# A quantized, low-rank-adapted double matrix product: another order for one strip's side work on TensorE, ScalarE and GpSimd

## The chip, the cores and the metric

The kernel runs on one core of one Trainium2 chip. The metric is device time in microseconds (us) of one execution. Before the change the median of 3 runs is 2667.78 us (2667.24 to 2671.78).

## What is computed

The reference, cut to what matters (x is 4096 tokens by 2048 in float32; `weight`, `W_base` are 2048 by 2048; the codebook has 32 values; lora rank 64; router of 8 experts with rank 16):

```python
lora_delta = lora_B @ lora_A * (32.0 / 64.0)
cb = codebook / max(abs(codebook))
wg = (weight + lora_delta).reshape(O, I // 128, 128)
normalized = wg / exp(scale_log)
quantized = cb[searchsorted((cb[:-1] + cb[1:]) * 0.5, normalized)]
w_q = ((quantized - normalized) + normalized) * exp(scale_log)
h = x @ (w_q + lora_delta).T                 # the conditioning layer
out = x + h @ W_base.T + b_base + 2.0 * routed_lora(h, A_w, cores, B_w, router_w)
```

`routed_lora` mixes 16 by 16 cores with a softmax over 8 experts. Nothing lies between the two large products but linear algebra, so the kernel first multiplies the two weight matrices (and adds the identity for the residual), and then multiplies x by the result.

## The kernel before, in words

**Two stages.** Stage A makes the combined weights, 16 *strips* of 128 input columns one after the other (`for i in range(NS)`, L755). Stage B (L873 on) multiplies x by them in 4 groups of 1024 tokens, each as 7 by 7 smaller products (two levels of a Strassen-like scheme) whose operands lie in `s_dram`. Stage A writes the combined strip blocks to `wc_dram`, and forms and writes the sums of blocks that stage B needs to `s_dram`.

**One strip of stage A** is a tile `w` of 128 by 2048 floats, normalized, and a tile `a` of the same size that becomes the quantized strip. The codebook has 31 thresholds. For a threshold r from 4 on, `raise_to` (L544) does two full-width instructions: ScalarE writes a *mask* of one byte per element (L549), VectorE then copies the next codebook value into `a` where the mask is set (L550). That is 27 mask steps; in what follows Mk is the step with r = 4 + k, so M0 to M26. There are 4 mask buffers (`mpool`, L431), so ScalarE can be at most four masks ahead of VectorE. From strip 6 on half of threshold 3 is one more, half-wide step in front of M0 (L556-557). The first codebook values and thresholds of a strip are made beforehand, during the strip before it, by other passes: ScalarE's three passes L516, L519 and L521 or L524 on a half strip (`scalar_level`), and GpSimd's pairs L534, L535 (`pool_levels`) and L539 (`last_level`).

**Side work during strip i.** The list `at` holds calls; `behind(k, f, ...)` has f's instructions recorded after the two instructions of Mk. Every engine runs its own instructions strictly in that recorded order (`tc.manual_schedule()`, L367); only semaphores hold engines against each other. The side work of strip i is:

- for strip i + 1: `load_w` (L391, two loads on SyncE's queue; there are two `w` tiles, so the tile is free only when strip i - 1 has read its `w` for the last time), `delta` (L404, the low-rank product of one half, 16 matmuls into the one PSUM tile `d`), `scaled` (L498, ScalarE takes `d` out into `a`, L502), `normalize` (L504, GpSimd adds it to `w`, L506, and divides, L429), then the first levels as above;
- for strip i - 1: `straight_through` (L564) has just been recorded behind M26 of strip i - 1: GpSimd does L572, L573, L574 on each half and so finishes the strip. Then TensorE multiplies the strip by the second weight matrix in four output blocks: `products` (L742) for blocks 2 and 0, four chunks c each, then blocks 3 and 1. Each takes a PSUM bank of three (`psum_m`); blocks 2 and 3 also use weight pieces that are streamed in (`load_piece`, L487). `keep` (L652) copies a block out on ScalarE (L654) and stores it to `wc_dram` (L655); `multiply_router`, `router_parts`, `router_sum` and `keep_router` do the same for the router columns, in another tile of the same PSUM pool;
- for strip i - 2: the last chunk of blocks 3 and 1 and its low-rank term (L609), in front of M0, then `route` (L674), and `keep` of blocks 3 and 1;
- from strip 5 on: one block of earlier strips is loaded (`begin`), its sums are formed by GpSimd (`outer_w`, L320; `inner_pair`, L329-332) and written to `s_dram` by SyncE's queue (`put`, L351-353).

**After strip 15** (L843 on) TensorE does the four blocks of strip 15. The first column sums are made on GpSimd (`first_fetch`, `first_make`, `first_put`). `late_columns` (L714) fetches blocks 0 and 2 of the last four strips from `wc_dram`, forms sums on VectorE and writes them from GpSimd's queue. `last_fetch` (L1179) does the same for blocks 1 (SyncE's queue) and 3 (GpSimd's queue) at the start of stage B. Of strip 15 `keep` stores from ScalarE's queue.

Of the kernel before, what the change touches and what calls it, by code (L numbers as in the profile page):

```python
# [28 lines left out]
NL = 4  # L29
# [154 lines left out]
def adaln_ffn_kernel(  # L184
# [29 lines left out]
    nc = tc.nc  # L214
    D, N = xT.shape
    NS, _, NM, _ = weight.shape
# [149 lines left out]
    with ExitStack() as sa:  # L366
# [22 lines left out]
        strips = {}  # L389
# [239 lines left out]
        def multiply_router(i):  # L629

            ps = psum_m.tile([P, OQ], F32, tag="m", name=f"m_{i}_r")
            for m in range(NM):
                j = m % 4
                nc.tensor.matmul(
                    ps[RP * j : RP * j + RP, 0:P], ra_sb[:, m, :], strips[i]["a"][:, m, :],
                    start=m < 4, stop=m >= NM - 4 and j > 0, tile_position=(0, RP * j),
                    skip_group_check=True,
                )
            nc.tensor.matmul(
                ps[0:RP, 0:P], lora_r, strips[i]["la"][:R], start=False, stop=True,  # L640
                tile_position=(0, 0), skip_group_check=True,
            )
            strips[i]["r"] = ps

        def router_parts(i):
            nc.scalar.copy(raw, strips[i]["r"][:, 0:P])

        def router_sum(i):

            nc.tensor.matmul(strips[i]["r"][:, P : P + RP], raw, stack, start=True, stop=True)  # L650

        def keep(i, b):  # L652
            out = spool.tile([P, 4, BC], F32, tag="out", name=f"out_{i}_{b}")
            nc.scalar.copy(out.rearrange("p q c -> p (q c)"), strips[i][b])  # L654
            (nc.scalar if i == NS - 1 else nc.sync).dma_start(wc_dram[i // 4][b][:, i % 4], out)  # L655

        def keep_router(i):
            nc.scalar.copy(rac[:, strip[i], :], strips[i]["r"][:, P : P + RP])
# [55 lines left out]
        def late_columns():  # L714

            t = big0.tile([P, NM, OQ], F32, tag="wb", name="late").rearrange("p m o -> p (m o)")
            for n, b in enumerate((0, 2)):
                f = t[:, 3584 * n : 3584 * n + 3584]
                columns(NK - 1, b, f[:, 0:2048], f[:, 2048:3584])
                fetch(NK - 1, b, range(3))  # L720
            for b in (0, 2):
                fetch(NK - 1, b, (3,))
            for b in (0, 2):
                if b == 0:
                    z = ypool.tile([P, 2048], F32, tag="up", name="late_z0")
                    z = (z[:, 0:1024], z[:, 1024:2048], t[:, 7168:8192])
                else:
                    more = ypool.tile([P, 1536], F32, tag="more", name="late_z1")
                    z = ypool.tile([P, 2048], F32, tag="up", name="late_z2")
                    z = (more[:, 0:1024], z[:, 0:1024], z[:, 1024:2048])  # L730
                last_outer(b)
                last_inner(b, (5, 6), z[0])
                last_inner(b, (2, 7), z[1])
                last_inner(b, (3,), z[2][:, 0:512])
                last_inner(b, (4,), z[2][:, 512:1024])
                last_put(b, (5, 6), (2, 7), (3,), (4,))
# [5 lines left out]
        def products(i, bs, c):  # L742

            for b in bs:
                multiply(i, b, c)
            if c == NC - 1:
                low_rank(i, bs)
# [7 lines left out]
        for i in range(NS):  # L755
            at = {}

            def behind(r, f, *args):
                at.setdefault(r, []).append(lambda: f(*args))

            if i > 1:

                products(i - 2, (3, 1), NC - 1)
                route(i - 2, 0)
                behind(0, load_route, i - 2, 1)
                behind(2, keep, i - 2, 3)
                behind(3, keep, i - 2, 1)
            if i + 1 < NS:
                delta(i + 1, 0)
                if i > 0:  # L770
                    behind(1, load_w, i + 1, 2)
                behind(4, scaled, i + 1, 0)
                behind(4, normalize, i + 1, 0)
                behind(10, scaled, i + 1, 1)
                behind(10, normalize, i + 1, 1)
                for r, f, parts in ((0, 0, (11, 12, 13)), (NL - 1, 0, (14, 15, 18)), (0, 1, (19, 20, 21))):
                    for n, p in enumerate(parts):
                        behind(p, scalar_level, i + 1, f, r, n)
                behind(14, pool_levels, i + 1, 0)
                behind(19, last_level, i + 1, 0)  # L780
                behind(21, pool_levels, i + 1, 1)
            if i > 0:


                behind(9, load_route, i - 1, 0)
                if i == NS - 1:
                    behind(9, load_route, i - 1, 1)
                for c in range(2):
                    behind(2 + 3 * c, products, i - 1, (2, 0), c)
                if i + 1 < NS:  # L790
                    behind(7, delta, i + 1, 1)
                if i > 1:
                    behind(8, route, i - 2, 1)
                for c in range(2, NC):
                    behind(2 + 3 * c, products, i - 1, (2, 0), c)
                behind(13, multiply_router, i - 1)
                behind(16, keep, i - 1, 2)
                behind(17, keep, i - 1, 0)
                for c in range(NC - 1):
                    behind((17, 20, 22)[c], products, i - 1, (3, 1), c)  # L800
                behind(19, router_sum, i - 1)
                behind(23, keep_router, i - 1)
                behind(18, router_parts, i - 1)
                if i + 2 < NS:
                    behind(20, load_la, i + 2)
            else:
                behind(3, nc.vector.reciprocal, rflat[:, NM:], flat[:, NM:])
                behind(7, delta, i + 1, 1)
                behind(22, lora_columns, 0)
                behind(24, lora_columns, 1)  # L810
                behind(25, lora_router)
            for n, (g, b) in enumerate(made.get(i, [])):
                step_of = (3, 5, 10, 13, 17, 23, 25) if len(made[i]) == 1 else (
                    (4, 6, 8, 9, 10, 12, 13) if n == 0 else (17, 19, 21, 22, 23, 24, 25)
                )

                def begin(g, b):
                    columns(
                        g, b,
                        ypool.tile([P, 2048], F32, tag="up", name=f"up_{g}_{b}"),  # L820
                        ypool.tile([P, 1536], F32, tag="more", name=f"more_{g}_{b}"),
                    )
                    fetch(g, b)

                def inner_pair(g, b, ms):
                    z = zp.tile([P, 1024], F32, tag="z", name=f"z_{g}_{b}_{ms[0]}")
                    inner_some(nc.gpsimd, g, b, ms, z)

                behind((0, 14)[n], begin, g, b)
                r = step_of  # L830
                behind(r[0], outer_w, nc.gpsimd, g, b)
                behind(r[1], inner_pair, g, b, PAIRS[0])
                behind(r[1], inner_pair, g, b, PAIRS[1])
                behind(r[2], put, g, b, PAIRS[0])
                behind(r[3], put, g, b, PAIRS[1])
                behind(r[4], inner_pair, g, b, PAIRS[2])
                behind(r[4], inner_pair, g, b, PAIRS[3])
                behind(r[5], put, g, b, PAIRS[2])
                behind(r[6], put, g, b, PAIRS[3])
            quantize(i, at)  # L840
            straight_through(i)

        last = NS - 1  # L843
# [11 lines left out]
        for bs in ((2, 0), (3, 1)):  # L855
            for c in range(NC):
                products(last, bs, c)
            if bs[0] == 2:
                multiply_router(last)
                router_parts(last)  # L860
            for b in bs:
                keep(last, b)
            if bs[0] == 2:
                router_sum(last)
                keep_router(last)
                late_columns()
        for h in range(2):
            route(last, h)
        for h in range(2):
# [262 lines left out]
    def store(t, g, ph, th, a, b):  # L1132
        c = HB * ph + NK * a
        to = outr[:, c : c + NK, (2 * g + th) * HT + b * QT : (2 * g + th) * HT + (b + 1) * QT]
        nc.sync.dma_start(to, blk(state[t, g], a, b))
# [14 lines left out]
    early, late, last = {}, {}, {}  # L1150
# [130 lines left out]
```

## Time and profile before

| | |
|---|---|
| median of 3 runs | 2667.78 us |
| the profiled execution, its own time | 2666.77 us |
| its span, first to last instruction | 2665.0 us |
| stage A to the end of strip 15's masks | 1172.5 us |
| from there to about 1290 us | blocks of strip 15, last columns, start of stage B |
| stage B after 1290 us | 1375 us, TensorE busy 1366.82 us |
| TensorE busy over the span | 2503.9 us (94%) |
| VectorE / ScalarE / GpSimd busy | 1549.0 / 1130.1 / 1367.2 us |
| mean granted TensorE clock | 0.975 |

The page cuts the span in 40 slices and gives each engine's busy share per slice in tenths. A group line names source line, engine, operation, output and input, then busy time, mean duration of one, and the idle time just before it with what ended it. A wait line names who waited for whom, the total, how many times, and the longest. A timeline line gives start and duration in us, and in brackets the idle time before it with its releaser. Ends of matmuls are modelled, and a busy TensorE need not be at its peak.

### The profile page before, as it was taken

What the parts mean: (1) busy time and instruction counts of PE and PEld (TensorE: products, weight loads), DVE (VectorE), ACT (ScalarE), POOL (GpSimd) and SP (SyncE); (2) the same over time, 40 slices, a digit from 0 to 9 for tenths busy, and PEclk for the clock granted to TensorE, in tenths of its full rate; (3) what the DMA queues carried; (4) which work ended last, traced back from release to release, by engine and by line L of the source; (5) the groups of instructions that cost most, each with busy time, mean ns of one, the idle gap of its engine ahead of it and who ended that gap; (6) DMA issues with size and microseconds to landing.
All of it is one profiled execution on the core that took longest, in us unless ns stands there. A gap on an engine that the chain in (4) does not pass through costs nothing.

```text
span 2665.0 us, 26423 instructions
## 1 busy us (share of the span) xinstructions
PE 2503.9 (94%) x10576; PEld 1704.1 (64%) x10576; DVE 1549.0 (58%) x990; ACT 1130.1 (42%) x796; POOL 1367.2 (51%) x783
## 2 busy tenths in 40 slices
PE   5499999999999999999999999999999999999999
PEld 2244444444444444345888888888888888888887
DVE  9999999999999999973433223242133332224221
ACT  7899999999999999930000000000000000000000
POOL 5777778889888888745313140042320323202224
PEclk9799999999999999999999999999999999999999
DMA  8255457776777777699844666536675455854554
GB/s 317 102 177 185 168 181 252 233 241 228 234 243 249 235 231 227 217 327 347 323 174 173 218 245 232 187 142 213 244 234 194 157 206 177 279 208 173 194 199 158
DMA packets 225979, 581.08 MB, mean 218 GB/s; under 512 B 20600, under 2 KB 121728, under 8 KB 182720
## 3 DMA queue, kind: packets, MB, share of 16 engines
q1 hardware_dynamic: 219296, 557.96, 61.1%
q0 software_dynamic: 4960, 14.95, 1.6%
q10 hardware_dynamic: 1600, 6.49, 0.7%
q8 instruction: 83, 1.36, 0.2%
q14 instruction: 40, 0.33, 0.0%
HBM read 477.62 MB, written 101.71 MB: 217 GB/s over the span
## 4 chain that ended last, share of the span: by engine, by line
PE 62%; ACT 17%; DVE 8%; POOL 7%; DMA 3%; issue 2%; SPq 0%; DVEq 0%; ACTq 0%; POOLq 0%
PE z L954 49%; ACT above L549 11%; PE m L621 10%; DVE a L550 7%; ACT sg L516 2%; ACT sg L519 2%; POOL a L572 1%; POOL a L573 1%; PE z L984 1%; ACT a L521 1%; POOL lv L534 1%; POOL a L574 1%; POOL a L535 1%; DMA xA<-in_xT 1%; DMA wc_dram<-out 1%
## 5 line engine op out<-in xcount | busy, mean ns | idle before, releaser
L550 DVE COPY_PREDICATED a<-above,step 128x2048 f32<-128x2048 uint8 (+1 forms) x448 | 1090.2, 2436 | 61.1 <-ACT above L549 19.3
L549 ACT ACTIVATE above<-w,neg_t 128x2048 fp8e5<-128x2048 f32 (+1 forms) x448 | 872.4, 1976 | 55.1 <-DVE a L550 44.5
L954 PE MATMUL z<-t,s 128*128 128x256 f32 x3584 | 791.4, 380 | 2.0 <-DVE u L1036 1.7
L954 PEld LDWEIGHTS z<-t,s 128*128 128x128 f32 x3584 | 677.5, 190 | 105.5 <-issue 13.2
L621 PE MATMUL m<-wbp,a 128*128 128x512 f32 x1024 | 502.1, 636 | 115.0 <-POOL a L574 101.0
L621 PE MATMUL m<-wb,a 128*128 128x512 f32 x1024 | 462.1, 594 | 4.4 <-ACT out L654 4.4
L621 PEld LDWEIGHTS m<-wbp,a 128*128 128x128 f32 x1024 | 202.6, 204 | 370.9 <-issue 239.7
L621 PEld LDWEIGHTS m<-wb,a 128*128 128x128 f32 x1024 | 194.5, 191 | 247.1 <-issue 242.4
L1034 ACT COPY m<-z 128x1024 f32<-128x1024 f32 x28 | 28.4, 1013 | 759.2 <-PE z L954 759.2
L1045 POOL TENSOR_TENSOR c<-u,m 128x1024 f32<-128x1024 f32 x16 | 50.1, 3130 | 443.8 <-DVE u L1042 422.4
L954 PE MATMUL z<-xA,s 128*128 128x256 f32 x1152 | 254.6, 379 | 0.0
L534 POOL TENSOR_SCALAR lv<-w,past,rise 128x1024 f32<-128x1024 f32 x65 | 245.9, 3783 | 3.7
L954 PEld LDWEIGHTS z<-xA,s 128*128 128x128 f32 x1152 | 218.8, 190 | 30.5 <-issue 0.8
L1045 POOL TENSOR_TENSOR M<-u,m 128x1024 f32<-128x1024 f32 x8 | 24.5, 3068 | 328.9 <-DVE u L1042 288.2
L954 PE MATMUL z<-xC,s 128*128 128x256 f32 x768 | 169.7, 379 | 0.0
L954 PE MATMUL z<-xB,s 128*128 128x256 f32 x768 | 169.7, 379 | 0.0
L535 POOL TENSOR_TENSOR a<-a,lv 128x1024 f32<-128x1024 f32 x65 | 154.3, 2374 | 27.1 <-ACT a L521 21.0
L1036 DVE TENSOR_TENSOR u<-z,m 128x1024 f32<-128x1024 f32 x28 | 34.3, 1224 | 218.5 <-issue 175.0
L1040 ACT COPY m<-z 128x1024 f32<-128x1024 f32 x28 | 28.3, 1011 | 308.8 <-PE z L954 308.8
L954 PEld LDWEIGHTS z<-xC,s 128*128 128x128 f32 x768 | 145.9, 190 | 19.8
L954 PEld LDWEIGHTS z<-xB,s 128*128 128x128 f32 x768 | 145.9, 190 | 19.8
L1042 DVE TENSOR_TENSOR u<-z,u 128x1024 f32<-128x1024 f32 x28 | 34.3, 1223 | 119.8 <-PE z L954 81.3
(213 smaller groups left out, 1958.0 us busy)
## 6 DMA issues: line engine op xcount, KB each, us to landing
s<-s_dram SPq DMA_DIRECT2D x196, 1024.0 KB, 4.9
wbp<-in_wbT SPq DMA_DIRECT2D x131, 1024.0 KB, 5.4
xs<-in_xT SPq DMA_DIRECT2D x64, 512.0 KB, 6.5
xA<-in_xT SPq DMA_DIRECT2D x24, 1024.0 KB, 9.4
s_dram<-z SPq DMA_DIRECT2D x84, 256.0 KB, 6.2
xB<-in_xT SPq DMA_DIRECT2D x16, 1024.0 KB, 10.4
outT<-M SPq DMA_DIRECT2D x16, 1024.0 KB, 12.5
w<-in_weight SPq DMA_DIRECT2D x30, 512.0 KB, 5.2
```

Of the source, the lines that this page charges most:

```text
L516: nc.scalar.activation(strips[i]["sg"], q, AF.Relu, bias=neg_t[:, r : r + 1], scale=GAIN)
L519: nc.scalar.activation(sg, sg, AF.Sign)
L534: v.tensor_scalar(lv, half(i, f, "w"), past[:, r : r + 1], rise[:, r : r + 1], ALU.is_gt, ALU.mult)
L535: v.tensor_tensor(a, a, lv, ALU.add)
L549: nc.scalar.activation(above[:, c], q, AF.Relu, bias=neg_t[:, r : r + 1], scale=GAIN, saturate=False)
L550: nc.vector.copy_predicated(a, above[:, c].bitcast(U8), step[:, r : r + 1].to_broadcast([P, F // n]))
L621: nc.tensor.matmul(ps, strips[i]["a"][:, CM * c + m, :], t[:, m, :], start=c == 0 and m == 0, stop=False)
L954: nc.tensor.matmul(z[:, c, :], s[:, k, ts(c, P)], rhs[:, k, :], start=not more and k == 0 and c % PER == 0, stop=k == NK - 1 and c % PER = ...
L1034: nc.scalar.copy(temp("m1", o), z["a"])
L1036: nc.vector.tensor_tensor(temp("u2", o), z["b"], state["m1", o], ALU.add)
L1042: nc.vector.tensor_tensor(temp("u3", o), z["d"], state["u2", o], ALU.add)
L1045: lambda d: nc.gpsimd.tensor_tensor(d, state["u3", o], state["m5", o], ALU.add),
```

## The change

It moves instructions to other places in the queues; no operation is added or removed. In each strip:

- `delta` of the second half moves from M7 to M1, and `scaled` moves from M4 and M10 to M1 and M3;
- `normalize` of both halves is recorded at M4 (before: M4 and M10), so on GpSimd both stand in front of `outer_w`;
- ScalarE's nine passes for levels move from M11-M15, M18-M21 to M7, M9, M10 (first threshold, first half), M12, M14, M15 (first threshold, second half), M19, M20, M22 (threshold 3, first half). `pool_levels` moves from M14 and M21 to M10 and M15, `last_level` from M19 to M22;
- `keep` of blocks 3 and 1 moves from M2 and M3 to M0 and M2; `keep` of block 0 from M17 to M18; the router's sum, parts and copy each move one step later;
- on GpSimd and SyncE's queue the seven steps of a block's sums move from M3, 5, 10, 13, 17, 23, 25 to M5, 12, 14, 16, 23, 24, 25.

After strip 15, copies out of PSUM (`evacuate`) and stores (`store`) are recorded apart: blocks 2 and 0 are both copied before the router's parts, their stores and `late_columns` come behind the first chunk of blocks 3 and 1, and blocks 3 and 1 are both copied before either is stored.

```diff
-        def keep(i, b):
+        def evacuate(i, b):
             out = spool.tile([P, 4, BC], F32, tag="out", name=f"out_{i}_{b}")
             nc.scalar.copy(out.rearrange("p q c -> p (q c)"), strips[i][b])
-            (nc.scalar if i == NS - 1 else nc.sync).dma_start(wc_dram[i // 4][b][:, i % 4], out)
+            strips[i]["out", b] = out
+
+        def store(i, b, q=nc.sync):
+            q.dma_start(wc_dram[i // 4][b][:, i % 4], strips[i]["out", b])
+
+        def keep(i, b):
+            evacuate(i, b)
+            store(i, b)
...
-                behind(2, keep, i - 2, 3)
-                behind(3, keep, i - 2, 1)
+                behind(0, keep, i - 2, 3)
+                behind(2, keep, i - 2, 1)
             if i + 1 < NS:
                 delta(i + 1, 0)
                 if i > 0:
                     behind(1, load_w, i + 1, 2)
-                behind(4, scaled, i + 1, 0)
-                behind(4, normalize, i + 1, 0)
-                behind(10, scaled, i + 1, 1)
-                behind(10, normalize, i + 1, 1)
-                for r, f, parts in ((0, 0, (11, 12, 13)), (NL - 1, 0, (14, 15, 18)), (0, 1, (19, 20, 21))):
+                behind(1, scaled, i + 1, 0)
+                behind(1, delta, i + 1, 1)
+                behind(3, scaled, i + 1, 1)
+                for f in range(2):
+                    behind(4, normalize, i + 1, f)
+                for r, f, parts in ((0, 0, (7, 9, 10)), (0, 1, (12, 14, 15)), (NL - 1, 0, (19, 20, 22))):
                     for n, p in enumerate(parts):
                         behind(p, scalar_level, i + 1, f, r, n)
-                behind(14, pool_levels, i + 1, 0)
-                behind(19, last_level, i + 1, 0)
-                behind(21, pool_levels, i + 1, 1)
+                behind(10, pool_levels, i + 1, 0)
+                behind(15, pool_levels, i + 1, 1)
+                behind(22, last_level, i + 1, 0)
...
-                if i + 1 < NS:
-                    behind(7, delta, i + 1, 1)
...
                 behind(16, keep, i - 1, 2)
-                behind(17, keep, i - 1, 0)
+                behind(18, keep, i - 1, 0)
...
-                behind(19, router_sum, i - 1)
-                behind(23, keep_router, i - 1)
-                behind(18, router_parts, i - 1)
+                behind(20, router_sum, i - 1)
+                behind(24, keep_router, i - 1)
+                behind(19, router_parts, i - 1)
...
-                behind(7, delta, i + 1, 1)
...
-                step_of = (3, 5, 10, 13, 17, 23, 25) if len(made[i]) == 1 else (
+                step_of = (5, 12, 14, 16, 23, 24, 25) if len(made[i]) == 1 else (
...
             for c in range(NC):
                 products(last, bs, c)
+                if bs[0] == 3 and c == 0:
+                    router_sum(last)
+                    keep_router(last)
+                    for b in (2, 0):
+                        store(last, b, nc.scalar)
+                    late_columns()
             if bs[0] == 2:
                 multiply_router(last)
+            for b in bs:
+                evacuate(last, b)
+            if bs[0] == 2:
                 router_parts(last)
-            for b in bs:
-                keep(last, b)
-            if bs[0] == 2:
-                router_sum(last)
-                keep_router(last)
-                late_columns()
+        for b in (3, 1):
+            store(last, b, nc.scalar)
```

## The prediction

> **What bounds the kernel now.** I read the page's 40 slices first, then its chain of waits, then the waits and timelines of single strips.
>
> ```profile
> PE   5499999999999999999999999999999999999999
> DVE  9999999999999999973433223242133332224221
> ACT  7899999999999999930000000000000000000000
> POOL 5777778889888888745313140042320323202224
> ```
>
> Up to slice 17 (1172 us) three engines look full; afterwards only TensorE is. The order of strip work matters in the first part alone. Which engine sets the pace there is told by who waits:
>
> ```profile
> DVE a L550 <- ACT above L549: 19.3, 49, 0.6
> ACT a L502 <- PE d L410: 49.8, 14, 5.5
> PE m L621 <- POOL a L574: 101.0, 15, 34.7
> ```
>
> VectorE waits 19.3 us in all of stage A: it is the bound, and what it waits for is ScalarE's masks. Its own step is 2.57 us (27 steps of strip 2 took 69.44). So a strip needs 69.4 us of VectorE (strips 1-5), 70.8 with the half step (6-15); the strips end at 100.7 (strip 0), 173.3, 243.0, 314.5, 386.1, 457.05 ... 1101.6, 1172.5: 71.5 from the third on. Why the masks come late shows in ScalarE's timeline of strip 9:
>
> ```profile
> 691.05 2.00 ACT L549 ACTIVATE above<-w,neg_t 128x2048 fp8e5<-128x2048 f32 x1 [0.57 <-DVE a L550]
> 696.54 1.02 ACT L502 ACTIVATE a<-d 128x1024 f32<-128x1024 f32 x1 [3.49 <-PE d L410]
> 697.46 1.99 ACT L549 ACTIVATE above<-w,neg_t 128x2048 fp8e5<-128x2048 f32 x1
> 699.36 1.14 ACT L516 ACTIVATE sg<-w,neg_t 128x1024 bf16<-128x1024 f32 x1
> ```
>
> At 691 it is four masks ahead (it waits for a free mask buffer), then stands 3.49 us at `scaled` because the second `delta` is behind two chunks of products. Then mask and level pass alternate, 2.9 us against VectorE's 2.57, and at 725 the lead is gone. ScalarE has about 66 us of work per strip, so only some 5 us of slack.
>
> GpSimd's start of a strip is the last view I need (strip 3 begins at 243.0):
>
> ```profile
> 243.01 2.38 POOL L572 TENSOR_TENSOR a<-a,w 128x1024 f32<-128x1024 f32 x1
> ...
> 252.22 2.37 POOL L573 TENSOR_TENSOR a<-a,w 128x1024 f32<-128x1024 f32 x1
> 254.67 1.90 POOL L574 TENSOR_TENSOR a<-a,scale 128x1024 f32<-128x1024 f32 x1
> 259.41 2.38 POOL L506 TENSOR_TENSOR w<-w,a 128x1024 f32<-128x1024 f32 x1 [2.85 <-DMA w<-in_weight]
> 261.87 1.90 POOL L429 TENSOR_TENSOR w<-w,rscale 128x1024 f32<-128x1024 f32 x1
> ```
>
> The next `w` is loaded only when the second L573 has read the old one (issue at 254.62). The waits of SyncE's own queue, from 457 to 1100 us, say it too:
>
> ```profile
> SPq L395 <- POOL a L573: 66.2, 9, 7.6
> ```
>
> So `normalize` begins 16.4 us after the strip began and the first half is normalized at 20.75. From strip 5 on the load's wait is hidden behind `outer_w` (5.1 us).
>
> **The change part by part.** E is the time at which VectorE ends the strip before; all times below are after E.
>
> *The first `delta` and `scaled`.* The 16 matmuls (1.09 us) leave TensorE's stream and run in its idle time before L574 is done (4.5 to 5.2 us per strip): hidden, and they end near 6.3, before the products' 6.9. ScalarE's 3.5 us wait goes. Alone that would be a gain.
>
> *`keep` of block 3 at M0.* The block is finished by TensorE about when the strip begins (strip 9's low-rank term: 742.44 + 1.13 against E = 743.5). In the new order products of (3, 1) cannot begin before the copy of block 2 at M16, about 45, wait 0.8 for the copy of block 0 (one step later), and take 28.95 (714.55 to 743.5): end at 74.7, 1.8 past the next E. ScalarE, 2 to 4 us ahead, stands at M0 until 1.8: copy 0.47, M1 ready at 4.3; copies and `scaled` (0.47, 0.91) follow between the next masks; M4 is ready at 12.3, and from there VectorE would start M8 at 12.3 + 4 x 2.57 = 22.6 (without any wait: 20.6, or 21.9 with the half step). So this wait alone already puts a strip at 22.6 + 19 x 2.57 = 71.4: no better than now.
>
> *The level pass at M7.* L516 for the first half now stands behind M7 and in front of M8. It needs the first half normalized. ScalarE gets to it at 18 to 20. `normalize` now comes before `outer_w`, so it meets the bare load: issue at 11.65, landing 4.75 later in strip 3 (3.9 to 6.0 over strips 1-5, median 4.7; 4.3 to 6.2 from strip 6 on, median 5.2 with both halves counted). I take 4.75 for strips 2-5 and 5.0 for 6-14: L506 starts at 16.4 or 16.65, L429 ends 4.35 later, at 20.75 or 21.0. Then L516 (1.04 to the next start), M8 (2.0) and the hand-over (0.04) give M8 to VectorE at 23.9 or 24.1. Queued behind L516 are all masks from M8 on, and VectorE waits for them. Nineteen steps are left: 48.9. The strip is **72.8** or **73.05**. The same wait was free before, because L516 stood at M11 (about 27.5).
>
> Here the Trainium skill speaks against my sum: "DMA: Bandwidth & Descriptors", the section on the anatomy of one DMA, gives about 2.0 us plus bytes/436e9 (fitted for GpSimd's path). The half load of 512 KB would then take 3.2, the half would be ready at 19.2, M8 at 22.3, and the 22.6 above would rule: 71.4, no change. The row says 4.75; I use the row.
>
> *Spread of the other passes.* From M8 on ScalarE starts with no lead. Masks cost it 1.91, passes 0.95 to 1.13, copies 0.47: counted in the new order the lead dips to -0.08 at M11 and 0.2 at M16 and ends at 2.7 after M26. So 0.1 us is lost and no more; without the spread it would be more, since VectorE is no longer covered.
>
> *GpSimd and SyncE's queue.* `normalize` ends at 25, `outer_w` at 30, the levels at 43 and 61, the last sums at 68, before 72.8: its 65 us fit. `put` now waits on SyncE for GpSimd's sums until about 48; behind it stand a block store and a weight piece needed three pieces (20 us) later: covered. The store of block 3 stands before `load_w`, but is released at 2.4, before 11.65. Cost nothing, up to 0.5 per strip if a store delays the load.
>
> *Sum for the strips.* Strip 1 (its load landed at 15.66): ends at 172.7, 0.6 earlier. Strip 2: 72.8 against 69.7, +3.1. Strips 3-5: +1.3 each, 3.9. Strips 6-14: 73.05 against 71.6, nine times 1.45, 13.1. Strip 15 has no next `w`, only the wait at M0: +0.2. Together +19.7.
>
> *After strip 15.* Before, ScalarE's store of block 2 held up the copy of block 0, and TensorE stood 4.43 us; the new order removes that and TensorE is done with the blocks some 6.5 us earlier. But:
>
> ```profile
> 1274.31 2.62 DVE L320 TENSOR_TENSOR last<-last 128x512 f32<-128x512 f32 x4 [9.12 <-DMA last<-wc_dram]
> 1288.53 7.17 PE L954 MATMUL z<-t,s 128*128 128x256 f32 x32 [1.71 <-DVE u L1036]
> ```
>
> Stage B's seventh product waits for VectorE, which is held by block 3's columns; their load was issued when the last sums of blocks 0 and 2 had landed, and these go back to the stores at 1214.72 and 1215.71. The new stores follow the first chunk (to 1214.2), the router's sum and copy: 1214.9 and 1215.3. So 0.4 us is gained, not 6.5. DMA engines are over 0.9 busy there and two loads move forward; bounds -6.5 and +3. I take -0.5, from the rows of the store.
>
> Total: 2666.77 - 0.5 + 19.7 = 2686 against the profiled execution; the median before lies 1.0 above that execution: **2687 us**.
>
> **Rivals.** *The spread works* (gain): if M8 and M0 do not wait, VectorE's gaps vanish: 5 x 69.45 + 10 x 70.8 = 1055 instead of 1071.8, and 2650 us. For it: ScalarE's work of 66 us fits in 70.8. Against it: it needs the half normalized by about 17.5 and the blocks finished before E, and neither row is near. *Neither* (no change): the load takes 3.2 to 3.6; then 71.4 per strip, strip 2 +1.7, 2668 us. *More waits* (slower still): the load takes 6.2 in every strip and the lead, being zero, is lost again at M11 and M16: 1.5 more per strip, 2707 us. That the change does not do what it says, because the passes queue up behind M7's wait, is the forecast itself.
>
> **Chances.** Forecast 0.78; its own range, landings of 4.3 to 5.8 and the ends of the tail, is 2676 to 2698. Gain 0.08, no change 0.09, more waits 0.05. The range 2668 to 2699 leaves out the gain, part of no change and the worst. A measurement tells about 0.2% (5.3 us) from no change: faster 0.08, same 0.09, slower 0.83.
>
> **What would show it.** Right: each strip 72.5 to 73.5 us; ScalarE waiting at L516 for L429 once per strip, 1 to 4 us, and VectorE then waiting 1 to 3 us for M8; GpSimd waiting 2.5 to 3.5 us for `w` in strips 6-14 too; ScalarE waiting at L654 for L609 at M0; no wait at L502; first product of stage B near 1258 (1238 plus the strips' 19.7), the seventh near 1308 and still held. Wrong: strips of 71.5 or less, or L516 without a wait, which would mean that `w` is there before 14.

## The result and the profile after

Before: 2669.78 us (median of 4 runs beside the changed kernel, 2667.24 to 2675.93). After: **2698.25 us** (4 runs, 2691.64 to 2699.94). The ratio is 1.0099, 95% interval 1.0073 to 1.0124: slower. The profiled execution after took 2691.64 us, the lowest of its runs, against 2666.77: +24.9. Its other three executions, 2697.66 to 2699.94 us, left no profile: the readings below account for the 24.9 us and not for the 28.5 between the medians, and where those three lose some 7 us more stays open. (One execution, of the kernel called level_8 below, ran at a granted clock of 0.736 and took 3357 us; it is left out.)

Slices of 67 us, after; to be held against the rows of before:

```profile
PE   5598989988889998899999999999999999999999
DVE  9999989999999999982523223232123322214321
ACT  7888988998888888950000000000000000000000
POOL 6677778898888888844404131032320323202224
```

In stage A, TensorE and ScalarE fall to 8 in many slices and VectorE in one, and VectorE's last strip reaches further into slice 17 (8 instead of 7). The waits of the first 1320 us say for what:

```profile
ACT out L654 <- PE m L609: 148.8, 17, 35.4
...
PE m L621 <- ACT out L654: 78.0, 15, 6.4
...
DVE a L550 <- ACT above L549: 42.8, 35, 4.0
POOL w L506 <- DMA w<-in_weight: 40.2, 14, 3.5
ACT sg L516 <- POOL w L429: 30.9, 15, 8.0
```

VectorE's wait for masks has risen from 19.3 to 42.8 us. The wait of `scaled` for `delta` (49.8) is gone. Two of ScalarE's waits take its place, once per strip: the copy of block 3 for TensorE (L654 for L609) and the level pass for GpSimd (L516 for L429). TensorE now stands for a copy (78.0) where it stood for GpSimd's L574 (101.0).

Strip 9 after runs from 684.4 to 757.0. GpSimd, then ScalarE, then VectorE:

```profile
700.67 2.38 POOL L506 TENSOR_TENSOR w<-w,a 128x1024 f32<-128x1024 f32 x1 [2.67 <-DMA w<-in_weight]
703.13 1.90 POOL L429 TENSOR_TENSOR w<-w,rscale 128x1024 f32<-128x1024 f32 x1
```

```profile
686.87 0.59 ACT L654 COPY out<-m 128x512 f32<-128x512 f32 x1 [5.63 <-PE m L609]
...
705.06 1.15 ACT L516 ACTIVATE sg<-w,neg_t 128x1024 bf16<-128x1024 f32 x1 [2.04 <-POOL w L429]
```

```profile
689.39 2.48 DVE L550 COPY_PREDICATED a<-above,step 128x2048 f32<-128x2048 uint8 x1 [1.21 <-ACT above L549]
692.20 15.39 DVE L550 COPY_PREDICATED a<-above,step 128x2048 f32<-128x2048 uint8 x6 [0.33 <-ACT above L549]
708.13 52.60 DVE L550 COPY_PREDICATED a<-above,step 128x2048 f32<-128x2048 uint8 x21 [0.54 <-ACT above L549]
```

L506 starts 16.2 us after the strip's start, when the load has landed; L516 follows at 20.6; VectorE gets M8 at 23.7. The gap in front of M8 is short, because VectorE has lost time before it: at M1, behind the copy of block 3, and at M2. Over strips 6 to 14 VectorE waits on average 1.9 us at M1, 0.3 at M2 and only 0.25 at M8 (in five of the nine strips, 0.6 at most). TensorE's line for the blocks of the same strip:

```profile
728.97 6.53 PE L621 MATMUL m<-wbp,a 128*128 128x512 f32 x8 [5.99 <-ACT out L654]
...
759.68 1.13 PE L609 MATMUL m<-lora_c,la 64*128 64x512 f32 x4
```

It stands 5.99 us for the copy of block 2 and then needs 6.53 us for eight matmuls that take 3.70 without a pause before them. So blocks 3 and 1 are done at 760.8, 3.8 us after the next strip has begun.

The last strip ends at 1196.84 (before: 1172.56), so the strips cost 24.3 of the 24.9 us of the profiled executions.

### The profile page after: what moved, and what is told of

Its sections match the earlier page's. It is cut to its first block, busy times and chain, and to the rows that moved or that the text cites. A ratio compares the mean times of both kernels' runs of the same rounds, so it can differ in the third digit from the quotient of the medians.

```text
span 2689.8 us, 26374 instructions
## 1 busy us (share of the span) xinstructions
PE 2508.9 (93%) x10576; PEld 1707.2 (63%) x10576; DVE 1547.4 (58%) x990; ACT 1123.9 (42%) x796; POOL 1367.3 (51%) x783
## 4 chain that ended last, share of the span: by engine, by line
PE 59%; DVE 16%; ACT 12%; POOL 6%; DMA 4%; issue 2%; SPq 0%; DVEq 0%; POOLq 0%; ACTq 0%
PE z L964 49%; DVE a L550 15%; ACT above L549 8%; PE m L621 7%; POOL a L573 2%; POOL a L572 2%; DMA w<-in_weight 2%; PE z L994 1%; ACT sg L516 1%; POOL w L506 1%; POOL a L574 1%; ACT sg L519 1%; POOL w L429 1%; ACT a L521 1%; DMA s_dram<-late 1%
## 5 line engine op out<-in xcount | busy, mean ns | idle before, releaser
L550 DVE COPY_PREDICATED a<-above,step 128x2048 f32<-128x2048 uint8 (+1 forms) x448 | 1089.0, 2434 | 86.6 <-ACT above L549 42.8
L549 ACT ACTIVATE above<-w,neg_t 128x2048 fp8e5<-128x2048 f32 (+1 forms) x448 | 863.6, 1971 | 21.9 <-DVE a L550 12.3
L572 POOL TENSOR_TENSOR a<-a,w 128x1024 f32<-128x1024 f32 x30 | 71.1, 2371 | 109.1 <-DVE a L550 109.1
```

What stands on the lines that cost most here:

```text
L549: nc.scalar.activation(above[:, c], q, AF.Relu, bias=neg_t[:, r : r + 1], scale=GAIN, saturate=False)
L550: nc.vector.copy_predicated(a, above[:, c].bitcast(U8), step[:, r : r + 1].to_broadcast([P, F // n]))
L572: v.tensor_tensor(a, a, w, ALU.subtract)
```

## The experiments

All times are medians beside runs of the kernel before on the same chip; "to before" is the difference of these two medians, and the intervals are of the ratio. Line numbers are those of the kernel after, unless said otherwise.

**tail_old.** The changed strips with the tail of before.

```diff
                 products(last, bs, c)
-                if bs[0] == 3 and c == 0:
...
             if bs[0] == 2:
                 multiply_router(last)
+                router_parts(last)
             for b in bs:
                 evacuate(last, b)
+                store(last, b, nc.scalar)
             if bs[0] == 2:
-                router_parts(last)
-        for b in (3, 1):
-            store(last, b, nc.scalar)
+                router_sum(last)
+                keep_router(last)
+                late_columns()
```

> The changed kernel with the tail of the kernel before (stores of the last strip's blocks straight behind their copies, router sum and late columns behind all of blocks 2 and 0); the strips are as changed. Theory A (two waits of ScalarE in each strip, the copy of block 3 and the level pass, cost all of it; the tail is worth under 1 us): 2695 to 2700 us, strip 15 still ending near 1196.8, the seventh product of stage B 115.5 to 117 us after it. Rival T (the new tail costs part of the loss, by stores that collide with the loads of the late columns): 2685 to 2692.

Measured: 2696.33 us, ratio 1.0092 (1.0078 to 1.0105), +24.5 to before. The strips end at 1197.55, the seventh product starts 116.7 after that. Rival T falls: the loss is in the strips.

**level_later.**

```diff
-for r, f, parts in ((0, 0, (7, 9, 10)), ...
+for r, f, parts in ((0, 0, (9, 10, 11)), ...
-behind(10, pool_levels, i + 1, 0)
+behind(11, pool_levels, i + 1, 0)
```

> The changed kernel with the first half's level passes at M9, M10, M11 instead of M7, M9, M10 (GpSimd's levels at 11 instead of 10). The wait for the normalized half is gone, the copy of block 3 stays at M0. Theory A (each wait alone is enough, since each covers the other): M1 still comes 5 to 6.3 us after the strip's start, and VectorE has 26 steps of 2.57 us left: strips of 72.0 to 73.1, in all 2682 to 2698. Rival L (the level pass at M7 is the cost, as predicted; the copy at M0 alone gives 71.4 per strip): 14 strips 1.8 shorter, 2673 or less.

Measured: 2660.79 us, 0.9958 (0.9945 to 0.9972), **-11.1 to before**. Moving three passes by at most two masks turns the loss into a gain. Waits of the first 1320 us:

```profile
ACT out L654 <- PE m L609: 120.6, 18, 38.3
...
ACT sg L516 <- POOL w L429: 13.4, 13, 2.5
...
DVE a L550 <- ACT above L549: 4.0, 9, 0.9
```

ScalarE still waits for TensorE at M0 (120.6 us in all, in the changed kernel 148.8); VectorE's wait is 4.0. So theory A falls: the wait at M0 is not enough by itself. Here the copy at M0 comes on average 0.4 us ahead of the strip's start, and ScalarE has the time.

**keep_later.**

```diff
-behind(0, keep, i - 2, 3)
-behind(2, keep, i - 2, 1)
+behind(2, keep, i - 2, 3)
+behind(3, keep, i - 2, 1)
```

> The changed kernel with the copies of blocks 3 and 1 at M2 and M3, as before the change, instead of M0 and M2; the level pass stays at M7. Theory A: M1 is in time, but M8 still comes 23.7 us after the strip's start, and 19 steps remain: strips of 72.5 to 73.0, in all 2685 to 2698. Rival K (the copy at M0 is the whole cost): strips of 71 or less, in all 2665 or less.

Measured: 2695.18 us, 1.0086 (1.0073 to 1.0100), +23.3. ScalarE in the strip from 758.4 on:

```profile
763.98 1.02 ACT L502 ACTIVATE a<-d 128x1024 f32<-128x1024 f32 x1 [6.16 <-PE d L410]
```

The edit took less away than intended: ScalarE now waits at `scaled`, because `delta` stands behind the same blocks in TensorE's stream, and VectorE's gaps are now at M2 and M4. Rival K falls in this form only; copy_earlier below is the cleaner test.

**both_later.** Both edits.

> The changed kernel with both edits: level passes at M9, M10, M11 and copies of blocks 3 and 1 at M2 and M3. Theory A: both waits are gone, VectorE has a mask ready nearly always: strips of 69.5 to 70 (2 to 5) and 70.8 to 71.3 (6 to 15), in all 2650 to 2665 us, at or below the kernel before. Rival S (the spread itself costs: ScalarE's lead is lost again at M11 to M16, or GpSimd's levels come late): strips of 72 or more, 2680 or more.

Measured: 2662.80 us, 0.9963 (0.9951 to 0.9976), -9.1. No better than level_later, so the place of the copies is worth nothing once the pass is later. The spread itself costs nothing that shows (rival S falls).

**level_8 and level_6.** The first pass one mask later, or sooner: a dose.

```diff
-((0, 0, (7, 9, 10)), ...
+((0, 0, (8, 9, 10)), ...        # level_6: (6, 9, 10)
```

> The changed kernel with only the first level pass of the first half one mask later: M8 instead of M7 (the passes are then at M8, M9, M10; GpSimd's levels stay at 10). Theory L (what the moved pass costs is the time until its half is normalized, 21 us after the strip's start, and then the pass and one mask; it holds the mask behind it only): now M9 comes at 24.1 and 18 steps of 2.57 us are left, 70.4, less than VectorE's own 70.8: strips of 70.8 to 71.3, in all 2658 to 2668. Rival A (the copy at M0 carries a part of it by itself): 2680 or more.

> The changed kernel with the first level pass of the first half one mask sooner: M6 instead of M7. Theory L: the same time of 24.1 us now holds M7, 20 steps are left: strips of 75.5, 14 times 2.57 us more, in all 2728 to 2736 us. Rival A: the two waits cover each other, so a part is hidden: 2715 or less.

Measured: level_8 2676.99 us, 1.0019 (1.0012 to 1.0026), +5.4; level_6 2727.16 us, 1.0207 (1.0190 to 1.0224), +55.5. level_6 behaves as theory L says: L506 still starts 16.2 us after the strip's start, M7 is handed over at 23.9 in the strip from 777.7, and the strips last 75.26 on average (forecast 75.5; the total is 0.8 under the forecast range). level_8 fits neither side.

**level_8_again.** The same kernel once more, for its trace.

> The kernel with the passes at M8, M9, M10 once more, for a profile at the full clock: it took 2675, not the 2658 to 2668 of theory L. That leaves about 1 us per strip over VectorE's own time. Theory L, completed: the wait still ends at M9 but leaves ScalarE with no lead, and the passes behind M9 and M10 then come before the next masks, so VectorE waits at M10 and M11 as well: strips near 71.9, VectorE's gaps of 0.5 to 1.5 us all between M8 and M12, none at M1. Rival A: the gaps are at M1, behind the copy of block 3.

Measured: 2676.76 us (one run). TensorE, then VectorE, in the strip from 748.3 on:

```profile
791.05 5.40 PE L621 MATMUL m<-wbp,a 128*128 128x512 f32 x8 [4.34 <-ACT out L654]
```

```profile
752.67 2.48 DVE L550 COPY_PREDICATED a<-above,step 128x2048 f32<-128x2048 uint8 x1 [0.60 <-ACT above L549]
755.48 68.31 DVE L550 COPY_PREDICATED a<-above,step 128x2048 f32<-128x2048 uint8 x27 [0.33 <-ACT above L549]
```

My completed theory was wrong, the rival's place was right: the gaps are at M1, behind the copy of block 3. TensorE stands 4.34 us for the copy of block 2, as in the changed kernel.

**copy_earlier.**

```diff
-behind(16, keep, i - 1, 2)
-behind(18, keep, i - 1, 0)
+behind(14, keep, i - 1, 2)
+behind(15, keep, i - 1, 0)
```

> The changed kernel with the copies of blocks 2 and 0 at M14 and M15 instead of M16 and M18: TensorE gets their PSUM banks back sooner, does not stand 5 to 6 us and is done with blocks 3 and 1 before the strip ends, so that the copy at M0 does not wait. Theory L: M8 still comes at 24 us; strips of 72.5 to 73.1, in all 2688 to 2698. Rival B (ScalarE stands for TensorE at M0 and so carries its delay into the next strip, and this is what makes the wait at M7 matter): 2675 or less.

Measured: 2701.03 us, 1.0110 (1.0095 to 1.0125), +29.4. ScalarE in the strip from 763.85, then VectorE:

```profile
784.23 1.15 ACT L516 ACTIVATE sg<-w,neg_t 128x1024 bf16<-128x1024 f32 x1 [6.91 <-POOL w L429]
...
803.82 0.59 ACT L654 COPY out<-m 128x512 f32<-128x512 f32 x1 [1.12 <-PE m L609]
```

```profile
787.30 17.99 DVE L550 COPY_PREDICATED a<-above,step 128x2048 f32<-128x2048 uint8 x7 [1.75 <-ACT above L549]
```

TensorE no longer stands, block 3 is done 4.3 us before the next strip, and there is no gap at M1. ScalarE comes to M7 earlier, waits the longer there (6.91), and M8 is handed over at 23.45 (23.7 on average over strips 6 to 14; 21.9 in level_later). So the wait at M7 is enough by itself to lose time: with 19 steps of 2.57 us left a strip is 72.5 us (an estimate), against 71.6 before. The strips lasted 73.8 and the time is above both forecasts; the cause that the trace offers is that M14 is too soon for the copy (1.12 us for TensorE), and VectorE has two more gaps, 1.04 and 1.01 us, behind M14 and M15.

**level_8_copy.** level_8 with those copies one mask sooner.

```diff
-behind(16, keep, i - 1, 2)
-behind(18, keep, i - 1, 0)
+behind(15, keep, i - 1, 2)
+behind(17, keep, i - 1, 0)
```

> The kernel with the passes at M8, M9, M10 and, besides, the copies of blocks 2 and 0 one mask sooner (M15 and M17). With the passes at M8 the second look showed VectorE's gaps at M1, 0.9 us per strip, behind a copy of block 3 that waits 5 us for TensorE, and TensorE itself standing 4.3 us for the copy of block 2. Theory L with a loop (the late pass makes ScalarE reach the copy of block 2 late, TensorE stands, and the copy at M0 of the next strip pays for it): with the copy one mask (some 2.9 us) sooner block 3 is done before the next strip, M1 is in time, and the time falls to 2660 to 2666 us. Rival (the passes at M8 to M10 are simply too close): 2673 to 2678, with the gaps behind M8.

Measured: 2662.43 us, 0.9964 (0.9950 to 0.9979), -9.1; VectorE's wait for masks falls from 23.6 us (level_8_again) to:

```profile
DVE a L550 <- ACT above L549: 10.9, 29, 0.8
```

The rival, with gaps behind M8 and 2673 us or more, falls. So the rest of level_8's loss was a loop through two engines and two strips: ScalarE late, copy of block 2 late, TensorE stands and restarts slowly, the copy at M0 of the next strip late.

**load_sooner.**

```diff
                 v.tensor_tensor(a, a, w, ALU.subtract)
                 v.tensor_tensor(a, a, w, ALU.add)
-                v.tensor_tensor(a, a, sc, ALU.mult)
+                if last:
+                    v.tensor_tensor(a, a, sc, ALU.mult)
+            for h in range(0 if last else n):
...
+                nc.gpsimd.tensor_tensor(a, a, sc, ALU.mult)
```

> The changed kernel with only GpSimd's last sums of a strip in another order: the two multiplications by the scale (1.90 us each) go behind the last read of the old weights instead of one of them in front of it, so the next load is issued 1.9 us sooner (9.75 instead of 11.65 after the strip's start); the level pass stays at M7. Theory L (load, normalized half, level pass, M8 is the chain that sets a strip): M8 comes 1.9 us sooner, strips of 71.0 to 71.5, in all 2665 to 2676; against that stands that the first half is ready for TensorE 4.7 us later. Rival (what matters is not the load, but that M7's pass stands in front of the masks in any case): 2690 to 2700.

Measured: 2688.65 us, 1.0057 (1.0042 to 1.0072), +16.1: 10 to 12 us less than the change, where theory L wanted 22 to 33. It met neither forecast and lies 1.4 us under the rival's range. A sooner load helps, but the trace shows two things that can have taken the rest; they were not tested apart. The load was issued 2.0 us sooner but L506 starts only 1.4 sooner on average (15.20 against 16.60): in strip 10 the load needed 6.5 us, beside column loads that were still under way. And the half that TensorE needs first came later, so blocks 3 and 1 were done 2.0 us into the next strip and M1 was late again.

**before_delta.** The kernel before with one part of the change.

```diff
-behind(4, scaled, i + 1, 0)
+behind(1, scaled, i + 1, 0)
+behind(1, delta, i + 1, 1)
+behind(3, scaled, i + 1, 1)
...
-behind(10, scaled, i + 1, 1)
...
-behind(7, delta, i + 1, 1)
```

> The kernel before with one part of the change alone: both halves of the low-rank product in front of the products, and ScalarE's two scaled copies at M1 and M3; level passes, copies, GpSimd's order and the tail as before. The prediction's step (ScalarE's stand of 3.5 us behind the second half goes, and this alone is a gain): strips between VectorE's own 69.5 (70.8 from the sixth on) and 71.5, in all 2654 to 2665 us. Rival (VectorE's gaps came from the level passes alternating with the masks, not from that stand): 2668 to 2674.

Measured: **2658.46 us**, 0.9946 (0.9932 to 0.9961), -13.2. VectorE from 731 us on, across a strip's border, has one line without any gap:

```profile
731.30 77.16 DVE L550 COPY_PREDICATED a<-above,step 128x2048 f32<-128x2048 uint8 x31
```

**delta_tail.** before_delta with the new tail as well.

> The kernel before with two parts of the change: the low-rank product and the scaled copies in front, and the new tail; level passes, copies and GpSimd's order as before. If the tail is worth less than 1 us, as in the changed kernel: 2655 to 2660. If the new tail's 6 us of TensorE count where the strips end sooner: 2650 to 2655.

Measured: 2659.05 us, 0.9950 (0.9938 to 0.9963), -13.5. The tail is worth nothing that can be told apart. These two are the fastest of all kernels here, though the intervals of level_later, both_later and level_8_copy overlap theirs.

**Side by side.** Means over strips 6 to 14, read from the timelines; the copy's time is counted from the start of the strip, "into the next" from the start of the next one (negative is ahead of it); the last column is the mean strip. The copy of block 3 starts only when block 1 is done too.

| kernel | L516 waits | copy of block 2 at | TensorE stands for it | blocks 3 and 1 done, into the next | VectorE's gaps behind ScalarE | strip |
|---|---|---|---|---|---|---|
| before | 0.00 | 42.0 | 0.73 | 0.1 | 0.95 | 71.6 |
| after (M7) | 1.71 | 44.3 | 5.78 | 3.1 | 2.56 | 73.2 |
| level_6 | 3.82 | 45.8 | 7.88 | 2.4 | 4.64 | 75.3 |
| level_8_again | 0.83 | 42.1 | 4.39 | 1.7 | 0.93 | 71.9 |
| level_8_copy | 3.09 | 40.2 | 0.65 | -0.5 | 0.18 | 71.2 |
| level_later (M9) | 1.02 | 40.2 | 1.06 | -0.4 | 0.10 | 71.1 |
| copy_earlier | 7.20 | 39.4 | 0.00 | -4.3 | 3.08 | 73.8 |
| before_delta | 0.00 | 39.3 | 0.00 | -1.4 | 0.05 | 71.0 |

The gap column explains the strip column: a strip without its gaps is 70.6 to 71.0 us in every row. ScalarE's own wait does not: level_8_copy waits longer at L516 than the changed kernel and loses almost nothing, since there the masks behind it are not yet due.

## Why the prediction was right, and where it was off

*First `delta` and `scaled`: right.* Alone a gain, 13.2 us. The reading of the timeline (3.5 us at L502 are the lead that is missing later) held: VectorE's gaps go from 0.95 to 0.05 us per strip.

*The level pass at M7: right, and the cause.* L506 at 16.6 (forecast 16.65), L516 at 21.0 (21.0), strips 6 to 14 at 73.2 (73.05). With the pass at M6, M7, M8 and M9 the times are 2727, 2698, 2677 and 2661 us, and copy_earlier shows that this wait needs no help. One sign of the prediction did not come: VectorE was to wait 1 to 3 us for M8 and waited 0.25 on average, since M1 and M2 had already cost it 2.3. The forecast took the longer of two waits, M8 at 24.1 by the pass and at 22.6 by the copy; measured, the gaps at M1 and M2 bring M8 to about 24 as well (on time at 21.9, plus 2.3). That the strip comes out as forecast although the gap is elsewhere is in part luck. What ties both gaps to the pass is level_later, where both are gone. "DMA: Bandwidth & Descriptors" of the Trainium skill, by which the load would have taken 3.2 us (an estimate) and nothing been lost, was rightly set aside: after, the loads of `w` took 4.3 to 6.2 us, median 5.0.

*`keep` at M0, "this wait alone already puts a strip at 71.4: no better than now": wrong.* Alone (level_later) strips 6 to 14 last 71.1 with hardly a gap. The failed step is that products of (3, 1) cannot begin before about 45: that was the time of a ScalarE without lead. With a lead, M16 is reached at 40, TensorE hardly stands (1.06 us), and block 3 is done before the strip ends. VectorE's gap at M1 follows from the late pass; it is not a cost of its own. Where both meet, another term was too small: I gave the blocks 28.95 us, read from a strip in which TensorE had stood only 0.73 us before them, and they took 31.8 (728.97 to 760.81), of which 2.8 is the slow restart after standing 6 us (last section); the prediction has no term for it. M1 then came at 6.3 in strip 10 instead of 4.3.

*The sum: right in kind, too small.* The strips cost 24.3 us instead of 19.7, and the medians differ by 28.5. The forecast was 2687 us with 2676 to 2698 as its own range; the median of 2698.25 lies 0.25 past its end, so the total came close only just. Read from the strip ends: strips 3 to 5 were 1.2 longer in all than forecast, strips 6 to 14 1.6 longer, and strip 15 1.6 longer (72.7; it has no next `w`, but the copy at M0 waits for TensorE there too).

*Spread of the other passes, GpSimd and SyncE's order: right,* together they cost little or nothing (none was tried alone): level_later carries them all, and with delta_tail's parts alone the kernel takes 2659.05, 1.7 less than level_later's 2660.79, which the intervals do not separate.

*The tail: right that it is swallowed.* Forecast -0.5, measured +0.5 (seventh product 116.5 after the last strip's masks, before 116.0, with the old tail 116.7 in tail_old); the sign is not settled by so little. TensorE is 6.4 us earlier at stage B, stands 4.24 us at 1273.9, and then stands for VectorE all the same:

```profile
1313.33 7.17 PE L964 MATMUL z<-t,s 128*128 128x256 f32 x32 [2.97 <-DVE u L1046]
```

*The rivals.* "The spread works" named the right condition, the half normalized by the time its pass is due, but there were two ways to meet it: an earlier load, or a later pass. Its 2650 lies 8 us under the best that was reached.

The account of the change, from medians to before: low-rank product in front -13.2; the tail about 0; other order of the side work about +2, not told from 0; the first half's passes at M7, M9, M10 instead of M9, M10, M11 about +36 to +40 (level_later against tail_old, measured together, and against the changed kernel): together about +25 to +29.

## What to carry to other kernels

An in-order engine that feeds the bounding one should get a side job only where its input is ready and its lead can bear the wait; read both times, counted from the start of the stage, and one place in the queue can decide between a gain and a loss. A wait that looks like a second cause may be the first one coming round the loop: take each away by itself, and look at the gaps of the bounding engine, not at the length of the waits. Moving a producer earlier gained less than its shift here (1.4 of 2.0 us in load_sooner).

## Not expected of the hardware

A slow restart of TensorE went into the loss. After standing 5.99 us eight matmuls took 6.53 us, after 4.34 us 5.40, and after 1.40 us of standing (with 16 small matmuls behind it) 3.70. The clock that the trace shows as granted over these rows is 0.56, 0.68 and 1.00; in the first row it is 0.50 up to about 734.7 and 1.00 from there. So 5.7 us of the row ran at half the clock; half of that is the 2.8 us lost. "TensorE: Matmul & The Clock Gate" of the Trainium skill, Part 1 on the clock gate, describes a half clock after a pause for about 3.4 us of work, which would lose 1.7 us (an estimate); the row of 5.40 lost that, the row of 6.53 lost 2.8. The mean granted clock shows little of it, 0.972 after and 0.975 before, because the kernel before has such a restart in nearly every strip too, at another place. Its strip 9, first the start of blocks 2 and 0, then that of blocks 3 and 1:

```profile
678.70 6.18 PE L621 MATMUL m<-wbp,a 128*128 128x512 f32 x8 [4.86 <-POOL a L574]
...
714.55 3.70 PE L621 MATMUL m<-wbp,a 128*128 128x512 f32 x8 [0.73 <-ACT out L654]
```

The granted clock over these two rows is 0.59 and 1.00. In the changed kernel the slow restart falls on the second pair of blocks, whose end the copy at M0 waits for; in level_later it is back at the first pair (6.31 us at 742.5). The row at 678.70 stood in the trace before the change, so the restart could have been put into the sum. How much of the loss it carries was not tested by itself.
